# A dearer hop in the planner of a list-scheduled graph layer, and gathers leashed to two engines in turn

## The chip, the cores and the metric

The kernel runs on one core of one Trainium2 chip. A core has five engines with an instruction queue each: TensorE (PE), VectorE (DVE), ScalarE (ACT), GpSimd (POOL) and SyncE (SP). Here SP issues the plain DMAs and POOL the indirect ones. The metric is the device time of one execution in microseconds (us); the median of three unprofiled executions is given, with the lowest and the highest.

## The reference

The input is a batch of 16 graphs with 1024 nodes and 64 channels, with a 0/1 adjacency of some 0.8% density. Each node's features are normalized and clipped at zero (`h`). From each node's neighbours some are dropped by a rule on their rank; over the rest, and the node itself, three quantiles per channel are taken and mixed; then come the node's own feature, a small MLP and the residual.

```python
rank = jnp.cumsum(ni, axis=-1) - ni                      # ni: neighbours, without the node itself
rem = neigh & (sk > 1) & (rank % sk == sk - 1) & mask[:, :, None]
rem = rem | jnp.swapaxes(rem, 1, 2)
nd = jnp.where(rem, 0.0, adj_) > 0
s = jnp.sort(jnp.where(nd[..., None], x[:, None, :, :], jnp.inf), axis=2)
...
for tau, w in zip((0.25, 0.5, 0.75), (0.25, 0.5, 0.25)):
    agg = agg + w * (v_lo + frac * (v_hi - v_lo))        # entries of s around tau * (count - 1)
out = x + agg
y = jax.nn.relu(out @ W1 + b1) @ W2 + b2
...
h = jnp.maximum(_layernorm(x, axis=-1), 0.0)
x = x + _L0_gnn_ref(h, adj, nodemask, ...)
```

## The kernel before

**The work.** `list_layer` handles the graphs one after another, two of them (a pair) at a time in the second half of the work. The 1024 nodes lie in 8 tiles of 128 rows.

Preparation of one graph is `load` (adjacency tile in, sign on ACT at L958, transposed on PE at L965, clipped to FP8 at L978), `number` (neighbour counts, L999 to L1022), `drop` (rank by PE at L1035 and L1040, distance by ACT at L1045, comparison by DVE at L1046 into `rem`), `keep` (PE at L1058 to L1063, clip by ACT at L1068 into `kept`, PE codes at L1071, copy by ACT at L1076 into `pack`), `order` (nodes sorted by their number of neighbours, a permutation `perm` by DVE at L1117) and `collect` (PE at L1138 and L1142, DVE's maxima into `keys` at L1151, ACT copies at L1155 to L1160, list entries `idx` on DVE to L1186). `normalize` writes the features to a table in DRAM, `gtab`.

The second half of the work of a pair is: `fetch`, which queues POOL's indirect DMAs (L1329), one per tile of nodes, slot of the list and graph, 952 in all, from `gtab` by `idx` into the list tiles `g`; `aggregate`, in which `sort` runs a pruned sorting network over the slots with DVE minima and maxima (L1434 to L1442), scales the wanted places (DVE L1459 or ACT L1457) and adds them up on PE (L1463); and `mlp`. The few nodes with long lists are set apart in `gg` and gathered and sorted by groups of eight graphs (L1681). For the last pair, PE picks part of the rows by one-hot matrices (`pick`, L1379 to L1410) in place of gathers.

**What sets the order.** The program text is not the order of execution. `arrange`, called at the end of `list_layer`, takes all instructions, makes a `Step` of each with a planned duration (`busy`) and a `lag` until others may see its result, finds the dependencies by tiles and buffers, and runs a list scheduler: `forward` starts each step when its predecessors allow it and its engine is free, by rank; `backward` walks from the end and gives new ranks. Six such rounds are made (`ROUNDS`), and the sequence with the shortest planned total is kept. It is then fixed for each of the five engines' queues, SP and POOL among them. The engines run their queues in that order, and semaphores still guard every dependency, so the plan decides the order, not the moment.

`between(s, o)` is the planned delay from the end of step s to the earliest start of a step o that depends on it: the lag of s plus 60 ns if the two are on different engines or s is a DMA; 115 ns between dependent DVE steps; else nothing. It is used in both walks. The lag is 200 ns for PE, 150 for ACT, 80 for DVE and 950 for a gather; a gather's planned time is 1345 ns.

Two further waits of the gathers are laid down in `arrange`. By `paced`, the k-th gather waits on a count of gathers already issued. By the leash, a gather waits for one step of DVE: of those DVE steps that another engine depends on (`tells`), the latest that ends in the plan more than 25 us (`LEASH`, 25000 ns) before the gather's own planned start. So POOL can't run ahead of DVE by more than about that much of the plan.

PSUM tiles are shared by tags: "mx" has three buffers and serves the tiles tp, cp, rk, kp and rowsT; "code" has two, for code and codeP; "agg" has two; "misc" one. In SBUF, `rem`, `perm` and `hot` share one buffer ("wide"). The list tiles `g` of the first two classes have two buffers, of the last two one.

`opened` places a small DVE memset (`pause`, L856) behind certain DVE instructions, 2043 in all.

Of the kernel before, what the change touches and what calls it, by code (L numbers as in the profile page):

```python
# [70 lines left out]
GROUP = 8  # L71
SLICE = P // GROUP
SECOND = 14
ROUNDS, LEASH = 6, 25000


TURNED = (0, 1, 3, 2, 0, 1, 3, 2)
# [590 lines left out]

def between(s, o):

    return s.lag + 60 if o.engine != s.engine or s.moves else 115 if s.engine == "DVE" else 0


def forward(steps, ranks):

    left, ready = [len(s.before) + len(s.behind) for s in steps], [0.0] * len(steps)
    starts, sequence, wire = [0.0] * len(steps), {e: [] for e in ENGINES}, [0.0]

    def place(s, when, free_to_go):
        starts[s.place] = when  # L680
        sequence[s.engine].append(s)
        end = when + s.busy
        if s.engine == "SP":
            wire[0] = max(wire[0], end) + s.load
            s.lag = wire[0] + 1500 - end
        for o in s.after:
            ready[o.place] = max(ready[o.place], when if s.place in o.behind else end + between(s, o))
            left[o.place] -= 1
            if not left[o.place]:
                free_to_go(o.place, ready[o.place])  # L690

    total = spread(steps, list(left), ranks, place)
    return sequence, starts, total


def backward(steps, starts):

    left, ready, ends = [len(s.after) for s in steps], [0.0] * len(steps), [0.0] * len(steps)

    def place(s, when, free_to_go):  # L700
        ends[s.place] = when + s.busy
        for p in (*s.before, *s.behind):
            o = steps[p]
            ready[p] = max(ready[p], when + s.busy - o.busy if p in s.behind else when + s.busy + between(o, s))
            left[p] -= 1
            if not left[p]:
                free_to_go(p, ready[p])

    spread(steps, list(left), [-(starts[s.place] + s.busy) for s in steps], place)
    return [-t for t in ends]  # L710


def arrange(tc, runs, loose, tails, paced):

    steps, found, number = [], {}, {}
    for ins in list(tc.nc.cur_bb.bb.instructions):
        if type(ins).__name__.startswith("BassTile"):
            continue
        if ins.name in tails:
            at = found[ins.name] = found[tails[ins.name]]  # L720
            at.tail.append(ins)
            number[ins.name] = len(number)
            at.busy += 12
            continue
        found[ins.name] = Step(ins, len(steps))
        steps.append(found[ins.name])

    written, read, users, order = {}, {}, {}, {}
    for s in steps:
        for u in s.reads + s.writes:  # L730
            name = u.tile.name
            for o, other in written.get(name, ()):
                if u.meets(other):
                    s.before.add(o.place)
            for o, other in read.get(name, ()) if u in s.writes or u.psum else ():
                if u.meets(other):
                    (s.before if u in s.writes or o.engine != s.engine else s.behind).add(o.place)
        for u in s.writes:
            for table in (written, read):
                table[u.tile.name] = [e for e in table.get(u.tile.name, ()) if not u.covers(e[1])]  # L740
            written[u.tile.name].append((s, u))
        for u in s.reads:
            read.setdefault(u.tile.name, []).append((s, u))
        for u in s.reads + s.writes:
            if getattr(u.tile, "tag", None):
                if u.tile.name not in users:
                    order.setdefault(u.tile.tag, []).append(u.tile)
                users.setdefault(u.tile.name, []).append(s)
    for tiles in order.values():
        for k, t in enumerate(tiles):  # L750
            bufs = t.tag_meta.bufs
            first = users[t.name][0]
            if k:
                first.behind.add(users[tiles[k - 1].name][0].place)
            if k >= bufs:
                first.before.update(o.place for o in users[tiles[k - bufs].name])
            for o in users[t.name][1:]:
                if o is not first:
                    o.behind.add(first.place)
    close = {found[n].place: (found[run[0]].place, found[run[-1]].place) for run in runs for n in run[:-1]}  # L760
    for s in steps:
        for first, last in {close[p] for p in s.before if p in close}:
            if not first <= s.place <= last:
                s.before.add(last)
    for s in steps:
        s.behind -= s.before
        s.before.discard(s.place)
        s.behind.discard(s.place)
        for p in (*s.before, *s.behind):
            steps[p].after.append(s)  # L770

    for s in steps:
        s.tells = any(o.engine != s.engine for o in s.after if s.place in o.before)
    ranks, best = [float(s.place) for s in steps], None
    for _ in range(ROUNDS):
        sequence, starts, total = forward(steps, ranks)
        if best is None or total < best[0]:
            best = total, sequence, starts
        ranks = backward(steps, starts)
    _, sequence, starts = best  # L780

    for k, s in enumerate(s for s in sequence["POOL"] if s.ins.name in paced[1]):
        if k > 1:
            paced[1][s.ins.name].wait_op(paced[0], k - 1, "sem-ge")
    shown = [s for s in sequence["DVE"] if s.tells]
    for s in sequence["POOL"]:
        while len(shown) > 1 and starts[shown[1].place] + shown[1].busy < starts[s.place] - LEASH:
            shown.pop(0)
        if s.ins.name in paced[1] and starts[shown[0].place] + shown[0].busy < starts[s.place] - LEASH:
            tc.add_manual_dep(  # L790
                s.ins, shown[0].ins.name,
                mybir.DependencyInfo(mybir.DependencyClass.Sync, mybir.DependencyReason.DATA),
                reason="leash of the gathers",
            )
    for steps in sequence.values():
        alike = iter(sorted((i for s in steps for i in s.tail), key=lambda i: number[i.name]))
        line = [i for s in steps for i in (s.ins, *(next(alike) for _ in s.tail))]
        at = {ins.name: k for k, ins in enumerate(line)}
        for ins in line:
            if ins.name in loose and at[loose[ins.name]] < at[ins.name] - 1:  # L800
                tc.declare_no_dep(ins, loose[ins.name], reason="read in order by one engine")
        for ins, then in zip(line, line[1:]):
            tc.add_manual_dep(
                then, ins.name, mybir.DependencyInfo(mybir.DependencyClass.NoSync, mybir.DependencyReason.DATA),
                reason="order of the engine",
            )
# [3 lines left out]
def list_layer(  # L810
# [682 lines left out]
    def aggregate(m, o, between=None):  # L1493
# [4 lines left out]
        for half in (0, 1) if last else (1, 0):  # L1498
            parts = CLASSES[2 * half:2 * half + 2][::1 if last else -1]
            for sides in ((0, 1), (1, 2)) if last and half else ((0, 2),):  # L1500
# [13 lines left out]
                if one is not None:  # L1514
                    yield from between(one, False)
# [314 lines left out]
    for m in range(pairs + 1):  # L1830
# [23 lines left out]
        weave(chain(results(m - 1) if m else (), (1.0,)), 140.0 if m else 1.0, side, 85.0 if m < pairs - 1 else 45.0)  # L1854

    arrange(tc, runs, loose, tails, paced)


# [185 lines left out]
```

## Time and profile before

| | us |
|---|---|
| median of three runs | 1444.05 (1441.54 to 1449.81) |
| the profiled execution | 1901.87 |
| its span, first to last instruction | 1900.1 |
| mean granted TensorE clock in it | 0.809 of full speed |
| POOL's first gather starts at | 63.1 |
| POOL's last indirect transfer ends at | 1855.8 |

The profiled execution is far longer than those without a profile. Shares of its span therefore don't carry over to the median as they stand; busy times of single instructions are the better guide.

By line, the costliest groups are: the gathers on POOL, 952 with 989.4 us busy; the sorts on DVE (L1437 and L1442), 659 instructions each and 621 us together; PE's codeP matmuls (L1142), 1024 with 191.7 us; and the three large groups of ACT, dist (256, 169.2 us), ne (248, 143.4 us) and kept (224, 133.4 us).

A busy time is the sum of an engine's instructions. An idle time is ascribed to the event that ended it; "issue" means that the profile shows nothing that was waited for, and "remote" a queue or core that it can't name. The share of the 16 DMA engines is 0.2 to 0.3 over most of the span.

### The profile page before, as it was taken

What the parts mean: (1) busy time and instruction counts of PE and PEld (TensorE: products, weight loads), DVE (VectorE), ACT (ScalarE), POOL (GpSimd) and SP (SyncE); (2) the same over time, 40 slices, a digit from 0 to 9 for tenths busy, and PEclk for the clock granted to TensorE, in tenths of its full rate; (3) what the DMA queues carried; (4) which work ended last, traced back from release to release, by engine and by line L of the source; (5) the groups of instructions that cost most, each with busy time, mean ns of one, the idle gap of its engine ahead of it and who ended that gap; (6) DMA issues with size and microseconds to landing.
All of it is one profiled execution on the core that took longest, in us unless ns stands there. A gap on an engine that the chain in (4) does not pass through costs nothing. (4 is left out here: it accounts for less than half of the span.)

```text
span 1900.1 us, 30251 instructions
## 1 busy us (share of the span) xinstructions
PE 1228.6 (65%) x8995; PEld 770.5 (41%) x9011; DVE 1226.8 (65%) x5869; ACT 1069.1 (56%) x2869; POOL 1027.3 (54%) x991
## 2 busy tenths in 40 slices
PE   6637566577867587667664687655873678733847
PEld 4424344254444344344432444433542345511434
DVE  5515277653676758774658658586757745596895
ACT  7646356466663578355662657353673675323765
POOL 0354564644564646554557455465565645577780
PEclk9769689597888798878877798767986789866868
DMA  5423232212331214121322123231230110112110
GB/s 185 137 76 92 61 92 67 83 50 68 84 102 43 86 39 137 42 73 45 102 79 50 54 47 104 54 94 32 54 71 18 31 21 20 19 23 49 27 31 15
DMA packets 128832, 121.67 MB, mean 64 GB/s; under 512 B 95730, under 2 KB 96274, under 8 KB 128658
## 3 DMA queue, kind: packets, MB, share of 16 engines
q1 hardware_dynamic: 97106, 87.29, 15.3%
q0 software_dynamic: 31552, 32.36, 8.7%
q8 instruction: 73, 1.20, 0.3%
q14 instruction: 101, 0.83, 0.1%
HBM read 108.79 MB, written 9.05 MB: 62 GB/s over the span
## 5 line engine op out<-in xcount | busy, mean ns | idle before, releaser
L1329 POOL DMA_INDIRECT g<-gtab,idx x952 | 989.4, 1039 | 816.3 <-issue 211.8
L1437 DVE TENSOR_TENSOR g<-g 128x384 f32<-128x384 f32 (+2 forms) x659 | 310.9, 492 | 25.1 <-issue 10.7
L1442 DVE TENSOR_TENSOR g<-g 128x384 f32<-128x384 f32 (+2 forms) x659 | 310.1, 491 | 10.1 <-DMA gg<-g 6.0
L1142 PE MATMUL codeP<-pack,perm 128*128 128x332 bf16 x1024 | 191.7, 332 | 59.2 <-DVE perm L1117 38.3
L1045 ACT ACTIVATE dist<-rk,bias 128x512 f16<-128x512 f32 x256 | 169.2, 701 | 84.5 <-remote 44.2
L1068 ACT ACTIVATE kept<-kp 128x512 fp8e4<-128x512 f32 x224 | 133.4, 600 | 132.9 <-remote 61.1
L978 ACT ACTIVATE ne<-tp 128x512 fp8e4<-128x512 f32 x248 | 143.4, 612 | 102.7 <-remote 67.4
L965 PE MATMUL tp<-kb,sg 128*128 128x128 bf16 x1024 | 119.9, 250 | 98.7 <-issue 37.5
L1463 PE MATMUL acc<-g,kf 128*128 128x128 f32 (+2 forms) x472 | 146.2, 446 | 55.7 <-ACT g L1457 35.5
L1035 PE MATMUL rk<-kb,cnt 128*128 128x512 bf16 x256 | 113.7, 444 | 93.6 <-ACT dist L1045 47.4
L1142 PEld LDWEIGHTS <-perm 128*128 128x128 bf16 x1024 | 100.1, 105 | 151.5 <-DVE perm L1117 49.4
L1040 PEld LDWEIGHTS <-ne 128*128 128x128 fp8e4 x1024 | 91.0, 110 | 154.7 <-issue 131.1
L1046 DVE TENSOR_SCALAR rem<-dist,half 128x1024 bf16<-128x1024 f16 x128 | 62.9, 493 | 129.4 <-ACT dist L1045 120.0
L965 PEld LDWEIGHTS <-sg 128*128 128x128 bf16 x1024 | 89.2, 113 | 140.8 <-issue 119.6
L1071 PE MATMUL code<-kw,kept 128*128 128x17 fp8e5 x1024 | 66.2, 175 | 122.4 <-ACT kept L1068 74.5
L958 ACT ACTIVATE sg<-at 128x1024 bf16<-128x1024 f32 x122 | 130.6, 1070 | 4.8 <-DMA at<-in_adj_dram 4.7
L1457 ACT ACTIVATE g<-g,coef 128x64 f32<-128x64 f32 x336 | 87.8, 339 | 79.0 <-DVE g L1437 44.1
L1058 PE MATMUL kp<-ne,kw 128*128 128x512 fp8e4 x256 | 112.7, 441 | 23.0 <-ACT cnt L1007 8.4
L1071 PEld LDWEIGHTS <-kept 128*128 128x128 fp8e4 x1024 | 54.1, 102 | 175.8 <-ACT kept L1068 98.6
L856 DVE MEMSET pause<- 128x1 bf16 x2043 | 120.5, 59 | 2.3 <-issue 2.3
L1463 PEld LDWEIGHTS acc<-g,kf 128*128 128x128 f32 x472 | 87.5, 224 | 84.0 <-ACT g L1457 43.1
L1040 PE MATMUL rk<-kw,ne 128*128 128x128 fp8e5 x1024 | 120.5, 245 | 0.0
(202 smaller groups left out, 2489.2 us busy)
## 6 DMA issues: line engine op xcount, KB each, us to landing
at<-in_adj_dram SPq DMA_DIRECT2D x122, 512.0 KB
g<-gtab,idx POOLq DMA_INDIRECT x952
xt<-in_x_dram SPq DMA_DIRECT2D x16, 256.0 KB
y<-in_x_dram SPq DMA_DIRECT2D x16, 256.0 KB
gtab<-xt SPq DMA_DIRECT2D x16, 256.0 KB
out_dram<-y SPq DMA_DIRECT2D x14, 256.0 KB
spare<-in_adj_dram SPq DMA_DIRECT2D x6, 512.0 KB
gg<-g SPq DMA_DIRECT2D x32, 48.0 KB
```

What stands on the lines that cost most here:

```text
L856: tails[nc.vector.memset(pause[:, at:at + 1], 0.0).ins.name] = ins.ins.name
L958: nc.scalar.activation(sg, at, AF.Sign)
L965: run.append(nc.tensor.matmul(tp[:, s], sg[:, m * P:(m + 1) * P], ident16, start=(s == 0), stop=(s == 3 and t // 4 != n), skip_group_check ...
L978: nc.scalar.activation(to, tp, AF.Relu, saturate=False)
L1040: run.append(nc.tensor.matmul(rk[:, s * P:(s + 1) * P], ne[:, 4 * n + s, ts], upper, start=False, stop=(s == 3), skip_group_check=True,))
L1045: nc.scalar.activation(dist[:, n * HALF:(n + 1) * HALF], rk, AF.Abs, bias=bias[:, t:t + 1])
L1068: nc.scalar.activation(kept[:, 4 * n:4 * n + 4], kp, AF.Relu, saturate=False)
L1142: run.append(nc.tensor.matmul(flat, perm[:, t, k * P:(k + 1) * P], pack[:, t], start=False, stop=(t == NT - 1), skip_group_check=True,))
L1329: ins = nc.gpsimd.indirect_dma_start(out=gathered[m, tiles][:, slot, k - lo, h], out_offset=None, in_=tables[2 * m + h][0], in_offset=bass ...
L1437: nc.vector.tensor_tensor(at(f + k * df, df, many), pa, pb, OP.min if what == "<" else OP.max)
L1442: nc.vector.tensor_tensor(pa if back else pb, pa, pb, OP.max if what == "<" else OP.min)
L1463: nc.tensor.matmul(acc, ident32, lines[:, s], start=False, stop=(s == now[-1] and not ends), skip_group_check=True)
```

## The change

Two edits in the planner. No instruction that computes is added, removed or altered.

The first replaces the constant 60 in `between` by `LATE`, 600 ns. Each planned hop between engines, and each planned delay behind a DMA, becomes 540 ns longer in both walks. The lags, the 115 ns of dependent DVE steps and the planned durations stay.

The second keeps two lists of anchor steps for the leash, one of DVE and one of ACT. At each step of POOL's sequence both are advanced by the same rule as before, the two lists change places, and a gather takes its anchor from the one in front. Gathers that follow one another are so bound in turn to a step of ACT and to one of DVE, each the latest that ends in the plan over 25 us before the gather's planned start.

```diff
-ROUNDS, LEASH = 6, 25000
+ROUNDS, LEASH, LATE = 6, 25000, 600
...
 def between(s, o):
 
-    return s.lag + 60 if o.engine != s.engine or s.moves else 115 if s.engine == "DVE" else 0
+    return s.lag + LATE if o.engine != s.engine or s.moves else 115 if s.engine == "DVE" else 0
...
-    shown = [s for s in sequence["DVE"] if s.tells]
+    leads = [deque(s for s in sequence[e] if s.tells) for e in ("DVE", "ACT")]
     for s in sequence["POOL"]:
-        while len(shown) > 1 and starts[shown[1].place] + shown[1].busy < starts[s.place] - LEASH:
-            shown.pop(0)
+        for shown in leads:
+            while len(shown) > 1 and starts[shown[1].place] + shown[1].busy < starts[s.place] - LEASH:
+                shown.popleft()
+        leads.reverse()
+        shown = leads[0]
         if s.ins.name in paced[1] and starts[shown[0].place] + shown[0].busy < starts[s.place] - LEASH:
             tc.add_manual_dep(
                 s.ins, shown[0].ins.name,
```

## The prediction

> **What bounds the kernel now.** I read the head line and the table of engines first, then the waits of GpSimd (POOL), then those of VectorE (DVE), then single gathers and single hand-overs in the timeline.
>
> ```profile
> span 1900.1 us, 30251 instructions
> PE 1228.6 (65%) x8995; PEld 770.5 (41%) x9011; DVE 1226.8 (65%) x5869; ACT 1069.1 (56%) x2869; POOL 1027.3 (54%) x991
> ```
>
> No engine is full in the profiled execution, and that execution (1901.87 us with what lies around the span) is 457.8 us longer than the median of the runs, 1444.05. Whatever is read from it has to be carried over to a run that has no such surplus. Where the surplus sits, the waits of POOL tell (engine, line, what was waited for: us in total, times, longest):
>
> ```profile
> POOL g L1329 <- issue: 211.8, 446, 14.1
> POOL g L1329 <- DVE g L1442: 69.4, 47, 12.7
> POOL g L1329 <- DMA g<-gtab,idx: 68.2, 198, 1.0
> POOL g L1329 <- DVE idx L1186: 62.3, 3, 61.2
> POOL g L1329 <- DVE pause L856: 59.4, 63, 5.6
> POOL g L1329 <- DVE num L1084: 30.4, 5, 12.3
> ...
> POOL g L1329 <- ACT hat L1223: 2.7, 1, 2.7
> ```
>
> All rows of that view that name DVE come to 519.3 us in 300 waits, those that name ACT to 4.4 us in 4. Undisturbed gathers follow one another like this:
>
> ```profile
> 92.52 0.94 POOL L1329 DMA_INDIRECT g<-gtab,idx  x1 [0.30 <-issue]
> 93.77 0.94 POOL L1329 DMA_INDIRECT g<-gtab,idx  x1 [0.30 <-issue]
> 95.02 0.94 POOL L1329 DMA_INDIRECT g<-gtab,idx  x1 [0.30 <-issue]
> ```
>
> So 1.25 us from start to start, of which 0.30 is a gap that even a free gather has. The reader should see that "issue" and "DMA" above are for the most part this gap (446 x 0.30 = 133.8 of 211.8; 198 x 0.30 = 59.4 of 68.2), while the DVE rows aren't: 519.3 less the head's 61.2 less 300 x 0.30 leaves 368 us in which gathers stood for DVE.
>
> Now POOL's floor. The first gather starts at 63.1 us and the last indirect transfer ends at 1855.8, which leaves a tail of 44.3. Between them a window sum gives 1026.1 us busy in 986 instructions, and 985 gaps of 0.30 are 295.5. Head, work, gaps and tail: 63.1 + 1026.1 + 295.5 + 44.3 = 1429.0 us. The span is 471.1 above it; the unprofiled median is 15 above it. I read this so: profiled, POOL is held by the leash to an overlong loop of the other three engines; unprofiled, it runs almost without a break and POOL is the bound, with DVE (1226.8 of 1444, 85% if its durations hold) close behind.
>
> The loop is in the waits of DVE:
>
> ```profile
> DVE rem L1046 <- ACT dist L1045: 120.0, 43, 19.0
> DVE num L1082 <- ACT pack L1076: 88.5, 11, 17.3
> DVE sk L1016 <- PE nb L1010: 56.2, 7, 23.3
> DVE keys L1151 <- PE codeP L1142: 45.5, 40, 4.3
> ```
>
> These are the steps of a batch's preparation (drop, keep, number, collect), which run PE, ACT, DVE, PE in turn. One wait is 2.8 us (120.0 / 43) or 8.0 us (88.5 / 11), far above a hand-over. What a hand-over itself takes shows where the consumer is alone:
>
> ```profile
> 53.95 0.48 DVE L1117 TENSOR_SCALAR perm<-turned,place_f 128x1024 bf16<-128x1024 f16 x1
> ...
> 54.49 0.11 PEld L1142 LDWEIGHTS <-perm 128*128 128x128 bf16 x2 [0.29 <-DVE perm L1117]
> ...
> 1887.92 0.59 ACT L1611 COPY highs<-high 128x512 f32<-128x512 f32 x1 [0.94 <-PE high L1585]
> 1888.55 0.69 DVE L1612 TENSOR_TENSOR highs<-highs,low 128x512 f32<-128x512 f32 x1 [0.84 <-ACT highs L1611]
> ```
>
> DVE ends at 54.43 and PE's load begins at 54.49; ACT ends at 1888.51 and DVE begins at 1888.55. A hand-over is 0.04 to 0.06 us. The old surcharge of 60 ns on top of the lag was therefore nearer to the chip than 600. The new value is no better price: it is slack, ordered into the queues.
>
> **What the Trainium skill says.** Perfetto Trace Analysis, section "Per-engine timelines", says that ACT, DVE and GpSimd are strict first-in first-out queues and that the semaphore's way to the other engine lies after the reported end. So one instruction placed too early stops all behind it. The trace agrees: the ACT copy st L1155 waits 82.8 us in 28 times for DVE keys, with unrelated evictions behind it. SBUF — State Buffer, section "Who interferes with whom", says that DVE and GpSimd share a port pair under an exclusive lock. That fits gathers of 1.13 us in stretches of DVE sorting (621 to 635 us) against 0.94 elsewhere, and it means that a denser DVE makes gathers dearer.
>
> **The change part by part.** (1) `between` adds 540 ns to each planned hop between engines and after each DMA. No instruction is added or removed; the five queues (SP's loads and POOL's gathers too) are re-sorted. A consumer becomes ready later in the plan, so other ready work goes ahead of it, and a chain with many hops gets a higher rank. Gain, bounded: each DVE wait on another engine or DMA can lose up to 0.54 us. Taking for every row of DVE's waits the smaller of its total and 0.54 x times, I get 118.6 us (rem 43 x 0.54 = 23.2, num 5.9, sk 3.8, keys 21.6, and so on). DVE waits less only where other work is to hand, and not all is on the path: half, 59 us, would turn the profiled 1901.87 into about 1843. In an unprofiled run POOL's floor caps it: 1444 - 1429 = 15 us if gathers cost what they cost in this trace. Lower bound of the effect: below nothing, rival D. I take 16, floor reached, hence 1428.
>
> (2) Steps moved. Gathers keep their order within a class, since their ranks follow the same buffers and lists; SP's 16 x 8 adjacency loads run two tiles ahead and ACT waits only 4.7 us in 4 times for them, so 0.54 more in the plan costs nothing unless a load is placed behind an output store that waits; then up to a load, 2.2 us (the longest such wait), a case. Taken as 0.
>
> (3) The leash. Each gather has one wait before and one after; every second anchor is now an ACT step whose planned end is 25 us back. Queued behind a waiting gather are all later gathers; who waits for them is the sort of the pair, which in this trace doesn't show a gather among its long waits. POOL is in order, so an ACT-bound gather may slip ahead of a DVE-bound one by one place, at best 1.25 us per stall, and the next one stops. ACT's own lateness (its longest waits are 22 to 23 us, below the 25 of the leash) can stop it anew. Bounds -10 to +10 us, taken as 0.
>
> (4) Head and tail (63.1 and 44.3 us) are dependent chains; order can hardly shorten them: 0, with 5 us either way.
>
> Sum: 1444.05 - 16 = 1428.
>
> **The rivals.** B, a larger gain: with steadier queues the gathers collide less, and their spacing moves from the mean 1.34 (1.04 + 0.30) toward 1.25. All undisturbed, POOL's floor is 63.1 + 985 x 1.25 + 44.3 = 1338.7; a third of the way from 1429 is 1399. For it: 0.94 is the commonest duration. Against: DVE must do the same 1227 us in less time. Time 1400.
>
> C, no change: only relative order matters; if all hops grow alike the sequences differ little, or POOL has no break left to lose. For it: the 15 us may be head and tail. Time 1444.
>
> D, slower: the ring of three PSUM tiles ("mx"). It serves tp, cp, rk, kp and rowsT: 256 + 32 + 256 + 256 + 28 = 828 tiles. In the plan a tile is now held by two dearer hops, and on ACT and DVE about one other instruction (some 0.6 us by the rows of ACT) stands ahead of each eviction for real. That is 828 / 3 x 0.6 = 166 us of later ring turns in the run, 10.4 us per batch. It is hidden while a batch's preparation has that much to spare against its gathers, 61.6 x 1.34 = 82.6 us per batch; below 10.4 us spare it decides, and each us missing costs 16. With 1.5 us missing: 1444 + 24 = 1468. For it: the preparation is what the profiled run waits for. Against: PE and ACT have over 200 us free in 1444.
>
> **How the numbers follow.** A measurement of this kernel can tell about 0.5% from no change, so 1437 to 1451 is "same". Chances: A (1428, own range 1415 to 1436) 0.40; B 0.18; C 0.16; D 0.26. Faster is A and B, 0.58; same 0.16; slower 0.26. The range 1390 to 1472 leaves out the lower third of B and the upper two fifths of D, some 0.16.
>
> **What would show it.** Right: in the profile after, the waits of rem on dist, num on pack and keys on codeP shrink, POOL's waits naming DVE fall below 368 + gaps, the profiled span falls by tens of us, busy sums stay within 2%. The leash: ACT rows appear among POOL's waits, and the sum of DVE and ACT rows doesn't fall by the leash alone. D would show as longer PE waits on ACT dist, kept and ne. I am wrong if the span after moves without those rows, if the unprofiled time falls below 1390, which needs cheaper gathers, or if the leash alone moves it by over 10 us.

## The result, and the profile after

| | before | after |
|---|---|---|
| median, us | 1445.86 (1441.54 to 1449.81, 4 runs) | 1468.34 (1467.82 to 1478.8, 4 runs) |
| ratio | | 1.0174 [1.0149, 1.0200] |
| span of the profiled execution | 1900.1 | 1466.9 |

The changed kernel is slower by 1.7%; 1428 was forecast. (The forecast's range, 1390 to 1472, contains the time; its direction is wrong.)

The two spans in the table must not be set against each other: the kernel before took 1441 to 1446 us (medians) in some sessions on the chips and 1905 to 1909 in others, without a profile too, and the profile shown of before has the length of a long session, while its times are from a short one. A short profile of the same kernel was taken later (run f1, below). Everything that follows on the cause of the 1.7% compares executions of the short kind. First the head line and the table of engines, of after and then of before in a short session:

```profile
span 1466.9 us, 30167 instructions
PE 1147.8 (78%) x9011; PEld 732.6 (50%) x9011; DVE 1218.0 (83%) x5869; ACT 1048.1 (71%) x2869; POOL 1056.5 (72%) x991
```

```profile
span 1438.5 us, 30251 instructions
PE 1099.7 (76%) x8995; PEld 707.3 (49%) x9011; DVE 1220.6 (85%) x5869; ACT 1041.3 (72%) x2869; POOL 1045.3 (73%) x991
```

DVE's work is the same; POOL is busy for 11 us more. The waits answer to those shown of before (engine, line, what was waited for: us in total, times, longest). After:

```profile
POOL g L1332 <- DMA g<-gtab,idx: 156.0, 512, 0.3
POOL g L1332 <- DVE idx L1189: 62.4, 3, 61.8
...
POOL g L1332 <- ACT dist L1048: 8.3, 17, 3.5
...
DVE g L1440 <- DMA g<-gtab,idx: 55.8, 17, 10.9
DVE keys L1154 <- PE codeP L1145: 33.0, 32, 2.2
DVE rem L1049 <- ACT dist L1048: 26.2, 18, 3.5
...
DVE num L1085 <- ACT pack L1079: 5.7, 5, 1.7
```

Before, in the short session (run f1):

```profile
POOL g L1329 <- DMA g<-gtab,idx: 133.3, 436, 0.5
POOL g L1329 <- DVE idx L1186: 61.5, 4, 60.6
POOL g L1329 <- DVE pause L856: 34.0, 110, 0.8
...
DVE rem L1046 <- ACT dist L1045: 29.1, 22, 2.6
DVE keys L1151 <- PE codeP L1142: 23.7, 36, 1.2
DVE num L1082 <- ACT pack L1076: 18.4, 7, 8.2
...
DVE g L1437 <- DMA g<-gtab,idx: 9.7, 3, 7.4
```

Apart from the head (`idx`) nearly every POOL wait is the 0.30 us gap between gathers: 156.0 / 512 = 0.30, 34.0 / 110 = 0.31. So POOL already ran without a break before the change, and the 368 us of gathers standing for DVE that the prediction read were a feature of the long session. After, the longest new wait of POOL is one of 3.5 us (for `dist` of ACT), so its waits don't hold the loss. It has to be looked for by place. Of the 986 indirect DMAs, counted from 0, number 98, 490 and 882 start at 188, 717 and 1243 us before and at 194, 718 and 1247 after: up to there 4 us are lost. Number 980 starts at 1398 and at 1412. Nearly everything is lost behind 1250 us, in the sort of the last pair and of the last group's lists `gg`, and in the tail. There the longest and the last gathers of before (run f1: start, us, engine, line, operation [idle before <- what ended it]):

```profile
1368.40 6.45 POOL L1329 DMA_INDIRECT g<-gtab,idx  x1 [0.30 <-DVE gg L1459]
...
1401.92 0.95 POOL L1329 DMA_INDIRECT g<-gtab,idx  x1 [0.30 <-DMA g<-gtab,idx]
...
1405.56 5.14 POOL L1749 DMA_INDIRECT out_dram<-gx,gto  x1 [1.46 <-DMA out_dram<-gx,gto]
...
1403.43 0.76 DVE L1437 TENSOR_TENSOR g<-g 128x256 f32<-128x256 f32 x2 [2.06 <-DMA g<-gtab,idx]
```

and of after:

```profile
1331.75 11.97 POOL L1332 DMA_INDIRECT g<-gtab,idx  x1 [0.30 <-DVE y L1663]
...
1412.94 0.94 POOL L1332 DMA_INDIRECT g<-gtab,idx  x1 [0.30 <-DMA g<-gtab,idx]
1414.19 0.94 POOL L1688 DMA_INDIRECT gx<-in_x_dram,gto  x1 [0.30 <-issue]
1415.44 0.94 POOL L1688 DMA_INDIRECT gx<-in_x_dram,gto  x1 [0.30 <-issue]
...
1420.86 7.46 POOL L1752 DMA_INDIRECT out_dram<-gx,gto  x1 [1.47 <-DVE g L1445]
...
1359.92 0.96 DVE L1440 TENSOR_TENSOR g<-g 128x768 f32<-128x768 f32 x1 [9.92 <-DMA g<-gtab,idx]
1417.91 0.29 DVE L1663 TENSOR_TENSOR gx<-gx,yp 128x128 f32<-128x128 f32 x1 [7.71 <-DMA gx<-in_x_dram,gto]
```

The whole loss can be read off four points of DVE and POOL:

| | before (f1) | after | difference |
|---|---|---|---|
| last list gather ends | 1402.87 | 1413.88 | +11.0 |
| DVE takes up work behind it | 0.56 later | 4.03 later | +3.5 |
| from there to the end of the sort | 14.4 (to 1417.80) | 24.0 (to 1441.93) | +9.6 |
| from there to the end | 20.7 | 25.0 | +4.3 |
| sum | 1438.5 | 1466.9 | +28.4 |

So the last gathers come later, and more of the sort lies behind them. The profiles suggest a cause for each. The gathers are late because some take 7 to 12 us in place of 0.94: what indirect DMAs of over 1.5 us take beyond 0.94 comes to 43.5 us after and to 31.7 in f1. The list gathers behind 1250 us have 33.2 and 25.1 of that, so 8 of the 11 us. And more sorting is left because DVE fell behind early (view: busy us of each engine by stretch, in the order PE, PE loads, DVE, ACT, POOL, each with its instructions, then clock, DMA share, GB/s). Before (f1), then after:

```profile
0.00:500.00 500.00, 415.23 (x3840) 265.44 (x3845) 407.29 (x1942) 417.90 (x1119) 337.13 (x335) 0.98 0.43 120
500.00:1200.00 700.00, 549.12 (x4454) 355.66 (x4461) 618.09 (x3202) 493.14 (x1375) 539.42 (x523) 0.90 0.31 77
1200.00:1475.00 275.00, 135.39 (x705) 86.18 (x706) 195.26 (x727) 130.26 (x376) 168.70 (x135) 0.78 0.13 27
```

```profile
0.00:500.00 500.00, 383.62 (x3344) 248.41 (x3345) 355.19 (x1639) 361.28 (x923) 334.09 (x333) 0.88 0.38 111
500.00:1200.00 700.00, 590.19 (x4621) 364.08 (x4620) 640.48 (x3362) 530.66 (x1503) 540.04 (x521) 0.93 0.31 84
1200.00:1475.00 275.00, 173.95 (x1049) 120.08 (x1047) 222.34 (x872) 156.14 (x444) 182.38 (x139) 0.79 0.13 28
```

DVE has 52 us less done at 500 us and still has 222 us to do behind 1200, 27 more than before. Its idle time in the first 500 us grew from 89.4 to 140.5 us. Of that, 28.4 us were waits for gathers, where f1 has none (over the run `g` L1440 waits 55.8 us in 17 times for gathers, against 9.7 in f1 for L1437, all of those behind 1340 us). A reading that fits, though no run shows the plan itself: with dear hops it holds the next preparation for not ready yet and puts the sort, which needs the gathers, in front of it on DVE's queue.

The granted clock of TensorE differs as well, 0.98 and 0.88 in the first 500 us. It does not account for the loss: behind 1200 us, where the time is lost, it is 0.78 and 0.79, and run h1, below, has 0.88 in the first stretch too and loses 0.2%.

### The profile page after: what moved, and what is told of

Same layout as the page of the kernel before. It is cut to its first block, busy times and chain, and to the rows that moved or that the text cites. A ratio compares the mean times of both kernels' runs of the same rounds, so it can differ in the third digit from the quotient of the medians.

```text
span 1466.9 us, 30167 instructions
## 1 busy us (share of the span) xinstructions
PE 1147.8 (78%) x9011; PEld 732.6 (50%) x9011; DVE 1218.0 (83%) x5869; ACT 1048.1 (71%) x2869; POOL 1056.5 (72%) x991
## 5 line engine op out<-in xcount | busy, mean ns | idle before, releaser
L1332 POOL DMA_INDIRECT g<-gtab,idx x952 | 1013.2, 1064 | 357.8 <-DMA g<-gtab,idx 156.0
L1440 DVE TENSOR_TENSOR g<-g 128x256 f32<-128x256 f32 (+2 forms) x659 | 312.3, 492 | 57.6 <-DMA g<-gtab,idx 55.8
L1445 DVE TENSOR_TENSOR g<-g 128x384 f32<-128x384 f32 (+2 forms) x659 | 311.1, 492 | 6.3 <-DMA gg<-g 5.4
L1145 PE MATMUL codeP<-pack,perm 128*128 128x332 bf16 x1024 | 183.0, 321 | 8.8 <-DVE perm L1120 8.3
L1466 PE MATMUL acc<-g,kf 128*128 128x128 f32 (+2 forms) x472 | 142.4, 423 | 31.6 <-DVE g L1462 14.4
L1038 PE MATMUL rk<-kb,cnt 128*128 128x512 bf16 x256 | 110.7, 433 | 36.7 <-ACT dist L1048 30.2
L1043 PE MATMUL rk<-kw,ne 128*128 128x128 fp8e5 x1024 | 115.4, 241 | 0.0
L1066 PEld LDWEIGHTS <-rem 128*128 128x128 bf16 x1024 | 80.1, 99 | 65.7 <-issue 9.3
L1158 ACT CAST st<-codeP 128x4 bf16<-128x4 f32 x128 | 21.3, 167 | 125.7 <-DVE rest L1156 84.9
L1061 PE MATMUL kp<-ne,kw 128*128 128x512 fp8e4 x256 | 99.3, 389 | 14.5 <-ACT kept L1071 9.9
L1466 PEld LDWEIGHTS acc<-g,kf 128*128 128x128 f32 x472 | 78.6, 210 | 53.2 <-ACT g L1460 20.7
L1066 PE MATMUL kp<-kw,rem 128*128 128x128 fp8e5 x1024 | 101.2, 222 | 0.0
```

Source lines behind the costliest of these rows:

```text
L1043: run.append(nc.tensor.matmul(rk[:, s * P:(s + 1) * P], ne[:, 4 * n + s, ts], upper, start=False, stop=(s == 3), skip_group_check=True,))
L1066: run.append(nc.tensor.matmul(kp[:, s], rem[:, t, at:at + P], minus, start=False, stop=(s == 3)))
L1145: run.append(nc.tensor.matmul(flat, perm[:, t, k * P:(k + 1) * P], pack[:, t], start=False, stop=(t == NT - 1), skip_group_check=True,))
L1332: ins = nc.gpsimd.indirect_dma_start(out=gathered[m, tiles][:, slot, k - lo, h], out_offset=None, in_=tables[2 * m + h][0], in_offset=bass ...
L1440: nc.vector.tensor_tensor(at(f + k * df, df, many), pa, pb, OP.min if what == "<" else OP.max)
L1445: nc.vector.tensor_tensor(pa if back else pb, pa, pb, OP.max if what == "<" else OP.min)
```

## The experiments

Each ratio is against the kernel before on the same chip. Runs e and k fell into sessions of the long kind, the others into the short kind.

**Is the surplus of 457.8 us one of the profile? (e1, f1: the kernel before, unchanged.)**

> The kernel before, unchanged, for a second profile. The profile of before was 1900 us long, its unprofiled time 1446; the profile of after was as long as its unprofiled time. Theory O (the order is fragile, and the profile upsets it): the profile is again far above 1446, with POOL waiting some 370 us for DVE. Theory X (that one profiled execution was disturbed from outside): the profile is 1440 to 1455 us long, POOL's gathers follow one another without a break, and the last gather ends by about 1395.

> The kernel before once more, beside the changed one on the same chip. In its profiles so far ACT waited up to 13 us for a releaser that the profile can't name (remote) while gathers ran without a break. Theory S (hand-overs are late on some executions of the chip, not of the kernel): if the kernel before takes 1440 to 1455 us here, those waits are gone and GpSimd's semaphore instructions take under 0.1 us each; if it takes some 1905, they are there again.

e1: 1909.68 us, ratio 1.0017 [0.9990, 1.0044], span 1905.8. f1: 1442.96, ratio 1.0000 [0.9984, 1.0015], span 1438.5. In both runs the profiled execution lies among the unprofiled ones, so a profile adds next to nothing in either session, and the surplus goes with the session. Why the first profile of before is long beside three short times isn't on record. The prediction took the surplus for the profiler's. f1's expectation holds too: the long waits of ACT are gone (last section), and POOL's semaphore instructions have a median of 0.04 us, against 0.70 in the profile of before.

**Each half of the change alone.** Late only keeps the first two hunks of the diff (`LATE` 600) and the old leash (both lists of anchors are of DVE); leash only keeps the third with

```diff
-ROUNDS, LEASH, LATE = 6, 25000, 600
+ROUNDS, LEASH, LATE = 6, 25000, 60
```

> The dearer hop alone; every gather stays bound to DVE. Theory H (the order made with the dearer hop costs the time): 1463 to 1473 us, as after, with the same gathers of 4 to 12 us beside the dense sort of the last pair. Theory L (the leash to ACT costs it): 1440 to 1450.

> The two leashes in turn with the old hop of 60. Theory H: 1440 to 1450 us, no difference that can be told from before. Theory L: 1460 to 1475.

> The changed kernel beside the kernel before. If the kernel before takes 1440 to 1455 here: 1463 to 1473, as measured. If it takes some 1905: theory S gives 1820 to 1870, the gain that the two leashes in turn brought alone (a factor of 0.965), less the dearer hop's loss (1.010); a factor of 1.017 as in the first measurement would give 1938 and speak against S.

> The dearer hop alone. If the kernel before takes 1440 to 1455 here: theory H 1463 to 1473, theory L (the leash to ACT costs the time) 1440 to 1450. If some 1905: 1912 to 1935, as in the first run of this edit.

> The two leashes in turn alone. If the kernel before takes 1440 to 1455 here: theory H 1440 to 1450, theory L 1460 to 1475. If some 1905: 1825 to 1850, as in the first run of this edit.

| | session | us | ratio |
|---|---|---|---|
| e2 late only | long | 1922.88 | 1.0098 [1.0060, 1.0137] |
| e3 leash only | long | 1836.84 | 0.9654 [0.9611, 0.9696] |
| f2 both (the change) | short | 1467.62 | 1.0166 [1.0131, 1.0200] |
| f3 late only | short | 1467.86 | 1.0168 [1.0140, 1.0195] |
| f4 leash only | short | 1441.75 | 1.0003 [0.9982, 1.0024] |

In the short session the dear hop is the whole loss and the leash does nothing. In the long session the alternating leash gains 3.5%: there the other engines are often late, and an anchor on ACT holds the gathers at other moments (this cause is argued, not shown). The effect of each half thus depends on the session, and the expectations of e2 and e3, made for short times, hold in f3 and f4 alone. The change as a whole wasn't run in a long session; the verdict is one on short ones.

**Does the leash matter at all? (e4.)**

```diff
-ROUNDS, LEASH = 6, 25000
+ROUNDS, LEASH = 6, 10**12
```

> The kernel before with no leash at all: gathers wait for their lists, for their buffers and for the count of gathers issued only. If the leash is what binds POOL in the runs of before, the gathers run up to 1.25 us apart from the start and end earlier; the time then moves by over 1% one way (less waiting: 1425) or the other (gathers crowd DVE: 1460). If POOL is busy without a break anyway, as the sum of the prediction had it, 1440 to 1450.

2549.42 us, ratio 1.3422 [1.3366, 1.3478], in a long session. The page's head line and POOL's waits of this run:

```profile
span 2547.8 us, 30228 instructions
PE 1215.0 (48%) x8995; PEld 762.8 (30%) x9011; DVE 1214.8 (48%) x5869; ACT 1059.3 (42%) x2869; POOL 978.0 (38%) x991
...
POOL g L1329 <- issue: 732.7, 818, 88.4
POOL g L1329 <- PE kp L1063: 125.3, 2, 106.4
```

None of the three expected times came. Without a leash POOL stands longer, in fewer pieces (41 gaps of over 0.35 us, where the profile of before has 268), though its work is cheaper (978.0 us). A free POOL doesn't make the kernel faster in a long session. No short session had this kernel.

**Where in the order does the dear hop hurt? (h1, h2.)** The program's loop over `m` runs to `pairs`, and the mark is set where `m == pairs - 1` begins, so that its last two rounds, with the sorts of the last two pairs, lie behind it. h1 takes 600 before that point and 60 from there; h2 the reverse. Both have the leash of the change.

```diff
-    return s.lag + LATE if o.engine != s.engine or s.moves else 115 if s.engine == "DVE" else 0
+    return s.lag + (LATE if s.place < TAIL[0] else 60) if o.engine != s.engine or s.moves else 115 if s.engine == "DVE" else 0
```

> The dearer hop for all steps up to the last two rounds of the program, the old hop of 60 for those after (the sort of the last two pairs and what follows). Theory E (DVE is starved early: the plan takes the preparation for slow, puts sorts that wait for gathers ahead of it, and the DVE work left undone makes the end late): where the kernel before takes some 1441, this takes 1455 to 1470, and DVE's busy time up to 500 us stays near 355 us against 407 of before. Theory T (only the order of the last 200 us is worse, with the late gathers of gx and DVE waiting 9 us for them): 1436 to 1448. Where the kernel before takes some 1905, the run tells nothing on this.

> The reverse: 60 up to the last two rounds, 600 after. Theory E: 1438 to 1448 us where the kernel before takes some 1441. Theory T: 1460 to 1470.

h1: 1448.43, ratio 1.0019 [1.0004, 1.0035]. h2: 1447.41, ratio 1.0015 [1.0002, 1.0028]. Neither the early deficit of DVE alone (h1 has it in full: 360.3 us of DVE work in the first 500) nor the dear hop in the last two rounds alone makes the loss. It takes both; what each theory had forecast for the half that it named, 1455 to 1470 and 1460 to 1470, didn't come.

**Which hops, and is it proportional? (h5, h7.)** h5 makes only the delay behind DMAs dear (`LATE if s.moves else 60`), h7 makes all hops 300.

> 600 only behind DMAs (gathers and loads), 60 between the compute engines. Theory E names the hops between PE, ACT and DVE in the preparation as the cause: 1438 to 1448 us where the kernel before takes some 1441. If the later landing of gathers in the plan is the cause: 1460 to 1470.

> Half the dearer hop, 300 everywhere. Theory E: the preparation of a graph gets too slow in the plan only from some hop on, since it has slack beside the gathers of a graph; at 300 little is lost, 1438 to 1450 us, no more than a third of the loss at 600. If the loss grows in proportion to the hop: 300 is 44% of the way from 60 to 600, so 1441 + 0.44 x 26 = 1452 to 1455.

h5: 1442.78, ratio 0.9998 [0.9962, 1.0034]. h7: 1443.25, ratio 0.9989 [0.9971, 1.0007]. With 300 there is no loss that can be told, so it doesn't grow in proportion to the hop. It sets in somewhere between 300 and 600; whether by a jump isn't shown. DVE's early deficit does come by degrees: at 500 us it has 394.1 us done with 300, between the 407.3 of before and the 355.2 of after. A surcharge in a planner selects a sequence, and of the sequences made with hops near 600 only this one was timed in a short session. That another of them, such as k3's with 590, would be free of the loss is not ruled out.

**Do the late loads of `gx` hold DVE? (k1, k2, k3, m1.)** After has a DVE wait of 7.71 us for `gx`, whose last two loads its plan puts behind all list gathers. k1 and m1 (the same kernel) rank them 80 us earlier in the changed kernel, k2 ranks them 40 us later in the kernel before, and k3 is the changed kernel with 590, whose plan puts them early by itself.

```diff
+        for s in steps:
+            if s.writes and s.writes[0].tile.name.startswith(("gx", "gto")):
+                ranks[s.place] += -80000.0
```

> The changed kernel, with the ranks of the steps that make the index gto and load gx raised by 80 us in the walks, so that POOL loads gx some 70 us earlier and the rest of the order stays much as it is. Theory G (the two loads placed last hold DVE, and with it the rest of the last sort): where the kernel before takes some 1441 to 1446, this takes 1440 to 1452. Theory B (the end is late because DVE has more left to do, whatever the place of gx): 1460 to 1470.

> The kernel before, with the ranks of the loads of gx lowered by 40 us, so that POOL loads gx last. Theory G: slower, 1452 to 1470 us, with DVE waiting for gx at about 1400. Theory B: 1438 to 1448.

> The changed kernel with a hop of 590 in place of 600. The plan comes out with gx some 65 us before its end, not last. Theory G: 1440 to 1453 us. Theory B, or a cost that grows with the hop: 1460 to 1470.

> The changed kernel with the loads of gx and their index raised by 80 us in the walks, as before. Where the kernel before takes some 1441 to 1446: theory G 1440 to 1452 us, theory B 1460 to 1470. Where it takes some 1905: 1880 to 1900, as measured, which tells nothing on G.

k1 (1891.12, 0.9903 [0.9877, 0.9929]), k2 (1919.47, 1.0045 [1.0022, 1.0069]) and k3 (1884.15, 0.9882 [0.9799, 0.9964]) fell into a long session, where POOL isn't the bound, and don't answer the question. m1 did: 1467.06, ratio 1.0146 [1.0100, 1.0191]. The wait is gone and most of the loss is still there:

```profile
1414.33 0.28 DVE L1666 TENSOR_TENSOR gx<-gx,yp 128x128 f32<-128x128 f32 x1
...
1423.50 0.94 POOL L1335 DMA_INDIRECT g<-gtab,idx  x1 [0.30 <-DMA g<-gtab,idx]
...
1410.69 0.43 DVE L1443 TENSOR_TENSOR g<-g 128x256 f32<-128x256 f32 x1 [8.10 <-DMA g<-gtab,idx]
```

Moved ahead to 1317, the two loads take some 4 us of POOL, and the list gathers behind them come later: the last now ends at 1424.4 in place of 1413.9, the rest of this being longer single gathers (one of 12.41 us at 1368). DVE waits 8.10 us for lists where it waited 7.71 for `gx`. On a POOL without gaps a DMA can only change places with another. The theory that the placing of `gx` is the cause falls.

**Work added to DVE at the end. (n1, n2.)** The last theory was that DVE's backlog of 27 us meets an end in which DVE stands. In n1 (the kernel before) and n2 (h2) each second half of a compare in the last group's lists `gg` runs twice in a row, outside the plan, so that the order stays:

```diff
                 others.append(gap(
                     nc.vector.tensor_tensor(pa if back else pb, pa, pb, OP.max if what == "<" else OP.min)
                 ))
+                if whole and list(lines.shape[2:]) == [C]:
+                    TWINS[nc.vector.tensor_tensor(
+                        pa if back else pb, pa, pb, OP.max if what == "<" else OP.min
+                    ).ins.name] = others[-1].ins.name
```

> The kernel before, its order unchanged, with one addition: in the last group's lists (gg, on DVE between 1285 and 1400 us) each of the 66 second halves of a compare (gg<-gg, 0.32 us) runs twice in a row. 66 x 0.32 to 0.38 us = 21 to 25 us more DVE work in the last stretch, without any other order. Theory S (the loss is a backlog of DVE, and in the last stretch the kernel before has some 25 us of DVE idle that takes it up, as it did in h1): 1445 x 1.00 to 1.005, at most 1452. Rival R (any work added to DVE at the end comes to the end, whatever the order): 1466 to 1470. Rival Q (DVE's backlog is not what counts, the loss is in what the tail's order makes POOL and DMA do): 1445.

> The kernel with the dear hop in the last iteration alone (h2, which ran in 1447.41 us) with the same 66 compares of gg run twice: 21 to 25 us more DVE work on top of an order whose tail has 20 us of DVE waits for gathers at 1340 to 1360 us, but 27 us less DVE work left at 1200 us than the changed kernel. Theory S (backlog times a tail in which DVE stands still): the slack is gone, so most of the added work comes to the end: 1460 to 1470. Rival R: 1468 to 1472, and n1 the same. Rival Q: 1447, and n1 1445. If n1 stays and n2 rises, S holds; if both rise, R; if neither does, Q.

n1: 1448.62, ratio 1.0052 [1.0032, 1.0071]. n2: 1448.79, ratio 1.0049 [1.0030, 1.0068]. None of the three theories had both numbers. The added work is 22 us (DVE behind 1200 us: 217.1 in n1, 195.3 in f1); n1 rises by 7.5 of it, n2 by 5 over h2 (0.34%). The profile says why: the experiment had a second effect that the theories hadn't counted. In h2, where neighbouring compares are mostly independent, DVE's instructions overlap (all 99 pairs of neighbours within `gg`'s compares do), and gathers beside them take far longer:

```profile
1322.67 0.37 DVE L1443 TENSOR_TENSOR gg<-gg 128x192 f32<-128x192 f32 x1
1322.93 0.31 DVE L1465 TENSOR_TENSOR gg<-gg,gcoef 128x128 f32<-128x128 f32 x1
...
1315.43 5.01 POOL L1335 DMA_INDIRECT g<-gtab,idx  x1 [0.30 <-ACT at_p L1570]
1320.74 12.32 POOL L1335 DMA_INDIRECT g<-gtab,idx  x1 [0.30 <-DVE y L1666]
```

In n2 the second run of a compare needs the result of the first and starts only behind its end (62 of 162 pairs of neighbours are so apart), and in such a stretch gathers run at nearly their undisturbed pace. Of those that start between 1310 and 1340 us n2 has 24, with a mean of 0.98 us and 1.12 at most, where h2 has 6 with a mean of 3.85:

```profile
1316.58 0.35 DVE L1455 TENSOR_TENSOR gg<-gg 128x192 f32<-128x192 f32 x1
1316.96 0.40 DVE L1458 TENSOR_TENSOR gg<-gg 128x192 f32<-128x192 f32 x1
...
1316.98 0.94 POOL L1342 DMA_INDIRECT g<-gtab,idx  x1 [0.30 <-DMA g<-gtab,idx]
1318.22 0.94 POOL L1342 DMA_INDIRECT g<-gtab,idx  x1 [0.30 <-DMA g<-gtab,idx]
```

The reader should see the starts: in h2 the second instruction begins 0.11 us before the first has ended (1322.93 against 1323.04), in n2 it begins 0.03 us behind (1316.96 against 1316.93). Indirect DMAs of over 1.5 us took 37.5 us beyond 0.94 in h2 and 7.3 in n2, and 31.7 in f1 against 11.3 in n1. The last list gather ends at 1385.0 in place of 1406.8 (n2), and at 1384.5 in place of 1402.9 (n1). Behind it DVE works for 38 and 40 us more to the end of the sort, where h2 and f1 have 14 and 15, and sets the end alone. So the added 22 us were, it seems, mostly paid for by earlier gathers, and the backlog theory in its simple form wasn't put to a clean test.

## Why the prediction was wrong

The forecast was 1428 and the time 1468.34. Of these 40 us, 16 are a gain that didn't come, and 24 a loss that the prediction's sum had put at nothing. Where the loss lies shows when the span of each short execution is split at the end of POOL's last indirect transfer:

| | last transfer ends | rest | span |
|---|---|---|---|
| f1, before | 1410.7 | 27.8 | 1438.5 |
| h1, dear hop up to the last two rounds | 1403.6 | 36.7 | 1440.3 |
| h2, dear hop in the last two rounds | 1421.6 | 24.1 | 1445.7 |
| after | 1428.3 | 38.6 | 1466.9 |
| m1, after with `gx` early | 1430.7 | 38.8 | 1469.5 |
| h7, a hop of 300 | 1402.3 | 35.8 | 1438.1 |
| n1 | 1411.1 | 35.2 | 1446.3 |
| n2 | 1408.4 | 39.4 | 1447.8 |

With the dear hop in the body alone the rest grows by 9 and the transfers end 7 earlier; in the last two rounds alone the transfers end 11 later and the rest is 4 shorter; with both the transfers end 18 later and the rest is 11 longer. That is the 28 us. These are single profiled executions: f2 repeats after with 1430.1 and 38.7, but h1's profile lies 6 us below its median, so most of its 7 us may belong to that execution, and h5's, with one indirect DMA of 23.27 us, lies 13 us above its own. The table shows where the time is. Why each half pays itself back alone and not together is argued from it: a late gather costs nothing where little sorting is left behind it, and much sorting costs nothing where the gathers come early.

Now step by step.

**The bound and its floor.** Right in kind: in f1 POOL has no break, and 62.5 + 1044.1 + 304.1 of gaps + 27.8 is the span. Wrong in size: the terms were read from the long session, and that the floor came out near is luck, since their errors partly cancel. In the short session gathers took 1044.1 and not 1026.1, and the tail 27.8 and not 44.3; the gap of a free gather is 0.305 us (f1's median), which makes 300.4 and not 295.5. With these terms the floor is 1434.8, only 3.7 below f1's span. The prediction also set a floor for the span against a median of whole executions, which are 1.8 us longer (1440.26 against 1438.5 in f1), and took 16 us where it had itself worked out a cap of 15. So of the 16 us of gain that the forecast rests on, some 4 were there to be had with f1's gathers, an estimate from these figures. The reading behind it, that the surplus was the profile's and that an unprofiled run had the same gathers, is refuted by e1 and f1. For the same reason its first sign, a profiled span shorter by tens of us, told nothing: the span shrank by 433 us while the kernel became slower.

**(1) The hop.** That DVE's waits could lose up to 118.6 us was no gain. (Some 11 us of that sum are waits of DVE for DVE itself, which a dearer hop doesn't touch.) Of the three rows that were to shrink two did, `num` on `pack` from 18.4 to 5.7 and `rem` on `dist` from 29.1 to 26.2, while `keys` on `codeP` rose from 23.7 to 33.0; but new waits for gathers came in, 55.8 us against 9.7. That a planned 600 is further from the chip than 60 was right. What the prediction missed is what such an error does to an in-order queue. The Trainium skill (Perfetto Trace Analysis, section "Per-engine timelines") was cited for the strict first-in first-out queues: an instruction that the plan holds to be ready late, and is in fact ready early, can lie behind one that must wait. The 55.8 us of DVE standing for gathers fit that; that the plan put them there for this reason is argued.

**(2) Moved steps at 0.** Right for POOL up to 1250 us: the gathers numbered above keep their times within 6 us. Not right for DVE, which lags by then, nor at the end.

**(3) The leash at 0.** Held: f4 is 1.0003, and in the profile after the longest wait of a gather on ACT is 3.5 us.

**(4) "Head and tail (63.1 and 44.3 us) are dependent chains; order can hardly shorten them: 0, with 5 us either way."** This is the step that failed. The head did stay (62.5 and 63.7). The tail grew from 27.8 to 38.6, and the last transfer, where it begins, ends 17.6 us later; 14 of these are lost behind 1250 us. The sentence asked only whether order can shorten the end. It can lengthen it: no later work fills a gap there, its sort carries no `pause` instructions (the last starts at 1308.7 us in f1 and 1316.6 after), and already in f1 nine of its indirect DMAs took 2 to 6.5 us apiece. Behind the sort's end the new order also leaves PE 16.3 us of matmuls, in place of 11.6. The sentence from the Trainium skill (SBUF — State Buffer, section "Who interferes with whom"), that DVE and GpSimd share a port pair under an exclusive lock, was cited for gathers of 1.13 us; in the end of this kernel the trace after shows 7.24, 11.97 and 6.79. h2 against n2, and f1 against n1, point to the overlapping, independent DVE instructions as what does it. That the lock is how they do it, no run shows.

**Rival D** gave the right side and, by chance, the right number (1468). Its sign came, weakly: PE's waits on `dist`, `kept` and `ne` of ACT are 100.0 us after and 82.3 in f1. But they aren't the loss, for h1, with the dear hop in all but the last two rounds, has 101.7 us of them and costs 0.2%.

What stays open: why some sessions are long; whether breaking up the dense sort of the last pair in the changed kernel itself brings its time back (n1 and n2 did that to the other orders only); whether it is this one sequence or any with a hop near 600 that loses; and why nothing is lost at 300. No kernel of the study is measurably faster than the kernel before in a short session.

## What to carry to other kernels

Before durations and floors are taken from a profile, see that its span agrees with the timed runs; where it doesn't, the whole table may be of another regime. A surcharge in a scheduler's model is not a cost but a choice of sequence: price a change of it by how far the end of the run can move, both ways. In this case the body with the new order alone cost 0.2%, and nearly all of the loss showed at the end. And where gathers on GpSimd run beside a VectorE sort, look at the single long gathers rather than at the mean.

## What the hardware showed that I had not expected

The kernel before had medians of 1441 to 1446 us in some sessions and of 1905 to 1909 in others, and the chip's number doesn't tell them apart: chips 0 and 11 had both. In the profile of before shown at the start, ACT waits with nothing named (258 us in 83 times, "remote"), and POOL goes on every 1.25 us meanwhile:

```profile
101.78 0.69 ACT L1045 ACTIVATE dist<-rk,bias 128x512 f16<-128x512 f32 x1 [9.29 <-remote]
115.80 0.60 ACT L978 ACTIVATE ne<-tp 128x512 fp8e4<-128x512 f32 x1 [13.34 <-remote]
...
101.26 0.94 POOL L1329 DMA_INDIRECT g<-gtab,idx  x1 [0.30 <-issue]
102.51 0.94 POOL L1329 DMA_INDIRECT g<-gtab,idx  x1 [0.30 <-issue]
```

f1 and the profile after have no such wait. Their cause wasn't found.

A single indirect DMA of POOL, 0.94 us when undisturbed, took 12 us (after) beside a dense stretch of independent DVE compares, 13.3 in h1 and 23.3 in the profile of h5, and went back to 0.98 us in the mean (n2, 1310 to 1340 us) where each second compare depended on the one before it.
